# Sixteen widths in steps of 16 slots, in place of eight in steps of 32, for the packed experts' branch trees

## The chip, the core and the metric

The kernel runs on one core of one Trainium2 chip. The metric is the device time of one execution in microseconds (us). All engines of the core are named as in the profile: PE is TensorE's matmul, PEld its weight load, PEq (or PEldq) the sequencer that reads TensorE's instructions, DVE is VectorE, ACT is ScalarE, POOL is GpSimd, SP is SyncE.

## What is computed

The reference is a decoder of two layers on an input of 2 x 1024 rows of 256 numbers, all in float32: a linear attention with a feed-forward block, a latent attention on a context, a recurrent cell, a causal attention, a cross attention, and at the end a mixture of eight experts. The change concerns the experts alone:

```
x = inputs.reshape(G, S, M)                      # 8 groups of 256 rows, M = 256
logits = einsum('GSM,ME->GSE', x, router_w)      # E = 8 experts
dispatch, combine = _gating_top2(logits, C)      # each row goes to 2 experts; C = 64 slots a group and expert
expert_inputs = einsum('GSEC,GSM->EGCM', dispatch, x)
layer_w0 = einsum('EGCM,EMH->EGCH', expert_inputs, w0_kernel)   # H = 1368
layer_w1 = einsum('EGCM,EMH->EGCH', expert_inputs, w1_kernel)
hidden = gelu(layer_w0) * layer_w1
expert_outputs = einsum('EGCH,EHM->EGCM', hidden, wo_kernel)
out = einsum('EGCM,GSEC->GSM', expert_outputs, combine)
```

An expert has 8 x 64 = 512 slots. How many of them hold a row depends on the data, since rows beyond the 64th of a group are dropped and groups may send fewer. Worked out from the reference's inputs, the eight experts fill 512, 512, 323, 393, 421, 337, 340 and 340 slots.

## The kernel before, in words

All work runs on one core, stage after stage, with the order of the instructions of each engine written out in the source (`manual_schedule`: an engine does its instructions in the order in which they were recorded). The last stage is the experts (class `Experts`, from L2432).

`Experts.run` (L2848) loops over the experts e = 0 to 7. For each it does eleven chunks of the hidden width 1368 (ten of 128 and one of 88, `HCH`). A chunk is `hidden`: `up` (L2914) multiplies the expert's inputs by the chunk of w0 and of w1 on TensorE, which gives two products side by side in one PSUM tile `ps_s`; `gelu` on ACT (L2944) reads the first, `mul` on DVE (L2948) multiplies it by the second and writes `hid`. There are two `ps_s` tiles in turn, so `up` of a chunk waits until `mul` of the chunk before the last one is done. After the eleven chunks `turned` transposes the next expert's inputs (L2765, eight small matmuls), and `outputs` (L2957) multiplies `hid` by wo: 44 matmuls, four blocks of 128 slots by eleven chunks. The rows go out to DRAM. wo of the next expert is loaded by SP as soon as the last output is done (L2521, L2522), w0 and w1 of the expert after the next one once the eleven chunks are done (L2513, L2514).

Experts 0 and 1 take all 512 slots. The rows of experts 2 to 6 are packed to the front of their 512 slots, and their number is known only on the chip: `counts` (L2718) reads it into TensorE's registers. So `up` of these experts is written once for each width of a list, `SIZES`, and a tree of branches picks the one to run:

```
L45    SIZES = (256, 288, 320, 352, 384, 416, 448, 512)
...
L2738  def sized(self, value, sizes, emit):
           if len(sizes) == 1:
               emit(sizes[0])
               return
           mid = len(sizes) // 2
           with self.k.tc.If(value > sizes[mid - 1]) as more:
               self.sized(value, sizes[mid:], emit)
           with more.Else():
               self.sized(value, sizes[:mid], emit)
...
L2933  self.sized(self.slots_n[e, 0], SIZES, lambda size: products(lambda t: t[:, :size]))
```

There are 55 such trees, five experts by eleven chunks. In TensorE's program a tree stands as follows: the branches and the bodies one behind the other, the widest body first. A body is 18 instructions: one that waits for the PSUM tile, eight weight loads and eight matmuls (four products, each a float32 matmul in two passes), and a jump to the end of the tree. A tree of eight widths is 7 compares and 8 bodies, 151 instructions; of these a run executes 3 compares and one body, and jumps over the rest. In the first two trees after some borders the waiting instruction is missing, and a body is 17. (`gelu` and `mul` take all 512 slots whatever the width.) Expert 7 has a smaller tree of its own (`WIDTHS`, L46), and the fourth block of the outputs of experts 2 to 6 stands in a single branch (L2888), which runs it if the expert has more than 384 slots; where it is skipped, the sequencer waits there until TensorE has finished what it has.

## Time and profile before

| | us |
|---|---|
| median of the 17 runs (1552.74 to 1563.68) | 1560.18 |
| the execution that was profiled | 1558.33 |
| span of its profile | 1556.5 |
| PE busy in the span | 1508.8 (97%) |
| first matmul of expert 2's trees, from the start of the span | 1265.05 |
| last matmul of expert 6's outputs ends | 1497.52 |
| matmuls L2922 on packed inputs (experts 2 to 7), busy | 172.7 |
| matmuls L2960 (all outputs), busy | 139.8 |

The profile is one execution. Busy time is given for each engine; a "releaser" is what ended an idle time. The float32 matmuls show as two records each, and their ends are modelled, so a record's mean duration is longer than its share of the engine: in a row of back-to-back matmuls the busy time divided by the count is the time that one takes of TensorE. TensorE's branches, waits and loads are the sequencer's; a branch has a record with a duration, but is not counted as busy. In the list of DMA queues, a queue of the kind "instruction" carries the programs of the engines; its queue q8 moved 102 packets of 16384 bytes in this execution. In a DMA answer for a stretch, the second line gives the GB/s in 40 equal slices of the stretch.

### The profile page before, as it was taken

The numbers are of one execution on the slowest core, as the hardware profiler recorded it, in microseconds if no ns is written. First come the engines' busy times: TensorE is split into PE (matmuls) and PEld (weight loads), VectorE is DVE, ScalarE is ACT, GpSimd is POOL, SyncE is SP. The second block draws the span as 40 slices with busy tenths as digits, with TensorE's granted clock in tenths as the row PEclk, the third lists the DMA queues.
The fourth block names the chain that finished last, engine by engine and source line by source line (L and its number), as shares of the span: only waits on it lengthen the run. The fifth ranks groups of instructions, "written<-read, shape, count | busy, mean of one in ns | idle before, by whom it ended". The sixth has DMA issues, their size and how long they took to land. (4 is left out here: it accounts for less than half of the span.)

```text
span 1556.5 us, 21057 instructions
## 1 busy us (share of the span) xinstructions
PE 1508.8 (97%) x8614; PEld 860.4 (55%) x8620; DVE 800.5 (51%) x1470; ACT 510.0 (33%) x782; POOL 288.8 (19%) x303
## 2 busy tenths in 40 slices
PE   7999999999999999999899999999999999999998
PEld 5756555444343344744354444455578476757787
DVE  8812653656554441696667778456762132111243
ACT  2231421433323332315556655644341111111110
POOL 2001320233221320121411111210033100000362
PEclk9999999999999999998899999999999999999999
DMA  6000000000000000010000000035003334232442
GB/s 257 0 0 4 0 0 0 1 1 1 1 0 1 0 31 0 1 36 1 1 1 2 1 1 1 1 128 179 1 33 135 93 135 137 95 105 79 160 143 89
DMA packets 37527, 72.42 MB, mean 47 GB/s; under 512 B 4568, under 2 KB 28312, under 8 KB 37016
## 3 DMA queue, kind: packets, MB, share of 16 engines
q1 hardware_dynamic: 28744, 53.21, 9.8%
q0 software_dynamic: 4704, 13.64, 2.7%
q10 hardware_dynamic: 3952, 3.70, 0.7%
q8 instruction: 102, 1.67, 0.4%
q14 instruction: 25, 0.20, 0.0%
HBM read 55.72 MB, written 14.81 MB: 45 GB/s over the span
## 5 line engine op out<-in xcount | busy, mean ns | idle before, releaser
L2922 PE MATMUL ps_s<-xe,w 128*128 128x352 f32 (+9 forms) x616 | 172.7, 442 | 2.9 <-ACT rows L148 1.8
L1720 PE MATMUL ps_s<-kT,qT 32*128 32x512 f32 (+3 forms) x768 | 163.3, 542 | 6.7 <-DVE mneg L1754 6.1
L2948 DVE TENSOR_TENSOR hid<-ga,ps_s 128x512 f32<-128x512 f32 (+3 forms) x99 | 62.1, 628 | 205.4 <-ACT ga L2944 205.4
L1900 ACT ACTIVATE pT<-ps_t 128x512 f32<-128x512 f32 x244 | 132.3, 595 | 106.7 <-PE ps_t L1834 106.6
L1834 PE MATMUL ps_t<-qT,kT 32*128 32x512 f32 (+3 forms) x656 | 160.9, 536 | 1.5 <-ACT pT L1900 1.4
L2922 PEld LDWEIGHTS ps_s<-xe,w 128*128 128x128 f32 (+1 forms) x616 | 108.3, 188 | 65.1 <-issue 31.7
L2960 PE MATMUL ps_o<-wo,hid 128*128 128x256 f32 (+1 forms) x638 | 139.8, 380 | 0.9 <-DVE hid L2948 0.9
L2960 PEld LDWEIGHTS ps_o<-wo,hid 128*128 128x128 f32 (+1 forms) x638 | 120.6, 190 | 17.9 <-DVE hid L2948 1.4
L2944 ACT ACTIVATE ga<-ps_s 128x512 f32<-128x512 f32 (+3 forms) x99 | 54.3, 549 | 197.5 <-PE ps_s L2922 194.8
L1107 DVE TENSOR_REDUCE part<-ps_s 128x2 f32<-128x1024 f32 x64 | 77.3, 1220 | 61.1 <-PE ps_s L1097 60.4
L1231 ACT ACTIVATE pT<-ps_s 128x1024 f32<-128x1024 f32 x64 | 65.5, 1023 | 114.4 <-PE ps_s L1224 114.4
L1720 PEld LDWEIGHTS ps_s<-kT,qT 32*128 32x128 f32 x768 | 63.0, 191 | 67.0 <-issue 35.6
L1754 DVE TENSOR_REDUCE part<-ps_s 128x2 f32<-128x1024 f32 x64 | 78.1, 1221 | 38.9 <-PE ps_t L1834 36.9
L1798 PE MATMUL ps_o<-pT,vr 128*32 128x256 f32 (+1 forms) x1280 | 92.3, 376 | 1.8 <-ACT oS L1812 1.8
L1847 POOL TENSOR_SCALAR_AFFINE_SELECT pT<-pT 128x512 f32<-128x512 f32 (+1 forms) x80 | 43.9, 551 | 248.6 <-ACT pT L1900 228.9
L1236 POOL TENSOR_TENSOR acc<-acc,pT 128x1024 f32<-128x1024 f32 x24 | 56.4, 2352 | 160.6 <-ACT pT L1231 152.4
L1754 DVE TENSOR_REDUCE mneg<-ps_s 128x2 f32<-128x768 f32 (+2 forms) x96 | 80.5, 867 | 2.2
L2922 PE MATMUL ps_s<-xin,w 128*128 128x256 f32 (+3 forms) x264 | 77.8, 452 | 0.0
L1834 PEld LDWEIGHTS ps_t<-qT,kT 32*128 32x128 f32 x656 | 72.2, 191 | 7.8 <-ACT pT L1900 3.9
L1798 PEld LDWEIGHTS ps_o<-pT,vr 128*32 128x32 f32 x1280 | 27.6, 110 | 81.0 <-issue 68.2
L1097 PE MATMUL ps_s<-kT,qT 64*128 64x512 f32 x256 | 70.3, 635 | 0.8 <-DVE part L1088 0.8
L1151 PE MATMUL ps_o<-pT,vr 128*64 128x512 f32 x256 | 69.4, 624 | 0.9
(453 smaller groups left out, 2318.7 us busy)
## 6 DMA issues: line engine op xcount, KB each, us to landing
w<-in_w SPq DMA_DIRECT2D x32, 684.0 KB, 6.8
wo<-in_wo SPq DMA_DIRECT2D x8, 1280.0 KB, 8.4
xi_rows<-xin SPq DMA_DIRECT2D x1, 3072.0 KB, 14.1
eo_rows<-rows ACTq DMA_DIRECT2D x12, 256.0 KB, 5.2
xr<-xi_rows POOLq DMA_DIRECT2D x6, 512.0 KB, 9.2
w_ffn<-in_w_ffn SPq DMA_DIRECT2D x1, 2304.0 KB, 13.9
x<-in_x SPq DMA_DIRECT2D x4, 512.0 KB, 6.5
w<-in_w_cell SPq DMA_DIRECT2D x2, 1024.0 KB, 16.9
```

What stands on the lines that cost most here:

```text
L1097: self.k.nc.tensor.matmul(s3[:, hh, :], lhsT=self.q[u][rows, qt * P : (qt + 1) * P], rhs=self.kt[u][rows, half * 512 : (half + 1) * 512], ...
L1107: self.k.nc.vector.tensor_reduce(self.part_of(u)[:, half, qt, :], s3, AX.X, ALU.max, negate=True)
L1151: nc.tensor.matmul(self.o[hh * 64 : hh * 64 + 64, :], lhsT=self.vr[b][:, kk, h * 64 : (h + 1) * 64], rhs=pT[:, hh, :], start=first, stop=last,
L1231: nc.scalar.activation(pT, s3, AF.Exp)
L1720: self.k.nc.tensor.matmul(s3[:, hh, at : at + n], lhsT=self.q[u][rows, qt * P : (qt + 1) * P], rhs=self.kt[u][rows, half * 512 : half * 51 ...
L1754: nc.vector.tensor_reduce(out, s3[:, :, at : at + n], AX.X, ALU.max, negate=True)
L1798: nc.tensor.matmul(self.o[hh * 32 : hh * 32 + 32, cols], lhsT=self.vr[b][:, kk, 4 * grp + hh, :], rhs=of(hh), start=fresh, stop=last and n ...
L1834: nc.tensor.matmul(out[:, at : at + n], lhsT=kt[rows, kk * P : (kk + 1) * P], rhs=q[rows, j * 512 + q0 : j * 512 + q0 + n], start=True, st ...
L1900: nc.scalar.activation(pT[:, hh, :], heads[hh], AF.Exp)
L2922: self.k.nc.tensor.matmul(cols(s[:m, i * 512 : (i + 1) * 512]), lhsT=wt[:, kc, at : at + m], rhs=cols(self.inputs[e][:, kc, first : 512]), ...
L2948: self.k.nc.vector.tensor_mul(self.hid[:m, hc, first : first + n], self.act.pop(hc)[:m, :n], self.now.pop(hc)[:m, 512 : 512 + n])
L2960: self.k.nc.tensor.matmul(o, lhsT=self.hid[:n, hc, st * P : (st + 1) * P], rhs=self.to[:n, hc, :], start=(hc == 0), stop=(hc == len(HCH) - 1),
```

## The change

One line is edited, the list of widths:

```
-SIZES = (256, 288, 320, 352, 384, 416, 448, 512)
+SIZES = (256,) + tuple(range(288, 513, 16))
```

The new list has sixteen widths: 256, then 288, 304, 320 and so on to 512. Nothing else differs in the source. In TensorE's program each of the 55 trees now has 15 compares and 16 bodies, 303 instructions where there were 151 (287 where the bodies have no waiting instruction); a run executes 4 compares and one body. From the first tree of expert 2 to the last branch of expert 6's outputs the program grows from 9254 instructions to 17558. The order of the instructions on all other engines is the same.

By their numbers of slots, experts 2 to 6 run these widths:

| expert | slots | width before | width after |
|---|---|---|---|
| 2 | 323 | 352 | 336 |
| 3 | 393 | 416 | 400 |
| 4 | 421 | 448 | 432 |
| 5 | 337 | 352 | 352 |
| 6 | 340 | 352 | 352 |

## The prediction

> **What bounds the kernel now.** I read the page's busy times first, then the groups by line, then the stretch of experts 2 to 6 (1265.05 to 1497.52 us of the span) by width of matmul, in order of time, by its branches and by its DMA queues.

> ```profile
> PE 1508.8 (97%) x8614; PEld 860.4 (55%) x8620; DVE 800.5 (51%) x1470; ACT 510.0 (33%) x782; POOL 288.8 (19%) x303
> ...
> L2922 PE MATMUL ps_s<-xe,w 128*128 128x352 f32 (+9 forms) x616 | 172.7, 442 | 2.9 <-ACT rows L148 1.8
> ```

> TensorE is the bound: 97% of the span, and before the 616 matmuls of the packed experts it idled 2.9 us in all. So a matmul that gets shorter there shortens the kernel, as long as TensorE's instructions arrive. The three widths that ran:

> ```profile
> L2922 PE MATMUL ps_s<-xe,w 128*128 128x352 f32 x240 | 72.1, 460 | 1.2 <-ACT rows L148 1.0 <-issue 0.2
> L2922 PE MATMUL ps_s<-xe,w 128*128 128x448 f32 x80 | 30.2, 539 | 0.0
> L2922 PE MATMUL ps_s<-xe,w 128*128 128x416 f32 x80 | 28.3, 514 | 0.8 <-ACT rows L148 0.8
> ```

> Busy by count gives what one costs TensorE: 300 ns at 352 columns, 354 at 416, 377 at 448, so 0.80 ns a column ((377.5 - 300.4) / 96). In order of time, expert 5's eleven trees are one unbroken run of 88 matmuls (these rows count two records for a float32 matmul), and expert 3's start after a short stall:

> ```profile
> 1309.83 31.06 PE L2922 MATMUL ps_s<-xe,w 128*128 128x416 f32 x88 [0.82 <-ACT rows L148]
> ...
> 1413.57 26.20 PE L2922 MATMUL ps_s<-xe,w 128*128 128x352 f32 x88
> ```

> Now the branches, all of them and then one alone:

> ```profile
> L2744 PEldq COMPARE_BRANCH  x286: 65/122/3234, 1261.2 to 1524.3; - x143
> ...
> L2744 PEldq COMPARE_BRANCH  x1: 1056/1056/1056, 1424.7 to 1424.7; - x1
> ```

> The columns are smallest, median and longest, in ns. The records come in few sizes: 65 for a compare that falls through, 214 for one that jumps, 176 for the jump that leaves a tree (each begins 58 ns after the end of the one before). But ten in experts 2 to 6 took 954 to 3234 ns. They are waits for code: the queue of the kind "instruction" shows as single slices of 27 GB/s, 16384 bytes in 0.6 us, once the weights have passed (window 1413 to 1437 us, the slices begin at 1422.6, 1426.2, 1429.2 and 1432.8):

> ```profile
> GB/s 0 0 0 106 189 270 333 375 336 299 372 389 77 10 22 20 27 0 0 0 0 0 27 0 0 0 0 27 0 0 0 0 0 27 0 0 0 0 0 0
> ...
> q8 instruction: 5, 0.08, 1.4%
> ```

> By the records the packet of 1423.01 landed at 1424.36. The branch of the second line above began at 1424.72 and ended at 1425.78, 1.41 us after that landing; the next packet started at 1426.51, 0.74 us after the branch's end. All ten long waits read so: the branch ends 1.34 to 1.55 us after a landing (1.40 in the middle), and the next packet starts 0.72 to 0.76 us after the branch, two late ones aside that I come back to. So **TensorE's sequencer has the page that it is in and the next one, and asks for a further page only when it enters the next**. A packet took 1.08 us in the mean of the 36 in experts 2 to 6. A page therefore can be had every 0.75 + 1.08 + 1.40 = 3.23 us at best; the nearest two packets of the whole span start 3.05 us apart. Experts 2 to 6 hold 9254 instructions and took 36 packets, so a page is 257 instructions, whether they are run or jumped over.

> Now a tree is 151 instructions, 0.59 pages: 1.9 us of supply, while TensorE works 2.4 to 3.0 us on it. The supply is hidden with 0.5 to 1.1 us to spare a tree, and single long waits are covered by the sequencer's lead of about a tree: the 1056 ns above lie inside expert 5's unbroken run.

> **The change, part by part.**

> Narrower products. Experts 2, 3 and 4 (323, 393, 421 slots) lose 16 columns: 88 x 16 x 0.80 = 1.13 us each, 3.4 us. Experts 5 and 6 (337, 340) keep 352. `gelu` and `mul` don't change.

> One compare more in a tree. It costs 65 + 58 = 123 ns where it falls through and 214 + 58 = 272 where it jumps; by the paths of the five counts a tree pays 0.12 to 0.42 us more. Nearly all of it lies under the sequencer's lead. Without the lead it shows: after a skipped fourth block (L2888, ahead of experts 3 and 6, where TensorE stands empty while the branches run, the 0.82 us above) and after the two groups of transposes in expert 2 (0.18 and 0.40 us idle by "issue"). Four places, at most 0.42 each: I take 1.0 us.

> [...]

> The pages. A tree becomes 303 instructions, 303 / 257 = 1.18 pages, so its supply takes 1.18 x 3.23 = 3.8 us. TensorE would need 2.3 us (336 columns) to 2.9 (432). **The trees become bound by the supply of code.** For one expert: nine trees of 303 and two of 287 are 3301 instructions, 12.8 pages. Two pages are there when it begins (the outputs before are 18 us of work on less than a page), so 11.8 intervals of 3.23 us remain: 38.2 us. Now the five take, from their first matmul to the end of the last, 28.7, 30.8, 33.0, 26.0 and 26.4 us, 144.9 together; then it is 191. The difference is 46 us, and it swallows both parts above: nobody gains from a shorter matmul that waits for its instruction. The outputs (L2960) have no such trees and don't change.

> [...]

> The load of wo. SP issues it at the start of each expert's trees (1280 KB, 8.4 us to landing). In each such window one page came late: its packet started 1.1, 3.8, 0.8, 4.0 and 2.0 us later than 0.75 us after the branch that entered the page before (at 1271.6, 1315.2, 1367.2, 1419.9, 1461.9), 2.3 us in the mean. Today that is covered. Afterwards a window of 8.4 us holds 8.4 / (3.23 + 2.3) = 1.5 such pages: 3.5 us an expert. I take 16 us in all; the bounds are 0 (the lateness was chance) and 5 x 2 x 4 = 40.

> Sum: the profiled execution took 1558.3; 1558.3 + 46 + 16 = 1620. The median of the runs is 1.9 us above that execution, so **1622 us** on its footing. With 3.05 us a page the 46 become 35; with packets of 1.5 us, as the slowest were, 3.65 us a page and 71. With the bounds of wo: 1595 to 1670.

> **The rivals.**

> *The clock falls.* Where TensorE stood empty for 2.4, 2.0, 2.2 and 1.8 us (at 691.4, 512.8, 752.6 and 1005.4) its granted clock went to one half within 4 us, for 17.1, 3.4, 10.2 and 3.4 us; after gaps of 1.4 and 1.2 us (771.3, 1143.2) it didn't.

> ```profile
> 690.00:694.00 4.00, 1.62 (x8) 0.67 (x7) 3.93 (x8) 1.08 (x2) 3.71 (x7) 1.00 0.59 191
> 694.00:711.00 17.00, 16.65 (x80) 9.19 (x79) 11.54 (x15) 4.06 (x8) 2.72 (x6) 0.50 0.00 0
> ```

> The columns end with the granted clock, the DMA share and GB/s. After the change a tree leaves TensorE empty for 3.8 - 2.4 = 1.4 us, below those gaps, but a late page makes it 3 to 5. Half clock costs a tree 4.7 instead of 3.8 us and doubles whatever outputs it reaches: between 2 and 8 us an expert. I expect an episode or two, inside the range; if every expert falls, 10 to 40 us more, 1632 to 1662, at the middle 1650.

> *The supply is quicker when it is pressed.* If a waiting sequencer, or a jump across a border, had two pages fetched at once, only part of the wait would stay: at half the loss, 1560 + 31 = 1591. For it: some packets in the list have no branch wait near them. Against it: under pressure (1461.9 to 1471.4) packets still came 3.06, 3.28 and 3.09 us apart.

> *The narrower products are what counts.* If a page came faster than TensorE uses one up, 2.3 / 1.18 = 1.9 us, the supply would stay hidden: 1560.2 - 3.4 + 1.0 = 1557.8 us, not slower than before, and a little under the 0.2% (3.1 us) that a measurement of this kernel can tell; with all compares hidden 1556.8, just beyond it. No interval in the span is under 3.05 us, which is why I give it little.

> **How the numbers follow.** Supply-bound trees as worked out: 0.70. The clock falling throughout: 0.14. Half of the supply hidden: 0.09. Narrower products alone: 0.07, of which 0.04 within 0.2% and 0.03 faster. The first three are slower by more than 0.2%: 0.93. The forecast is the first case's 1622. The range goes from 1590, which takes in pages at 3.05 us with wo at nothing and touches the third case, to 1660, which takes in the most of the second; the corners left out, with the fourth case, are about 2 in 10.

> **What would show it.** Right: about 134 packets on q8 in place of 102 (17558 / 257 is 32 more), in the trees 3.0 to 3.5 us apart; 341 branch records in place of 286, some fifty over 0.9 us in place of ten; the 88 matmuls of expert 5, with the same width as before, stretched from 26 to 35 to 42 us and broken by about one "issue" gap a tree; PE busy well below 97%, the outputs of an expert still 15 to 19 us. Wrong: packets under 2.5 us apart in the trees, or expert 5's run still at 26 us. If packets are as forecast but TensorE has no gaps, the lead is longer than I read it. If the granted clock shows long halves in the trees, it is the first rival.

## The result, and the profile after

The changed kernel takes 1633.31 us in the median of 8 runs (1628.99 to 1637.89), the kernel before 1559.65 in the median of 46 (1552.14 to 1565.07): a ratio of 1.0474, 95% interval 1.0456 to 1.0492, 73.7 us slower. The profiled execution took 1634.48 us with a span of 1632.7.

The page of the changed kernel, the lines that answer to those of before, and the queue that carries the code:

```profile
PE 1530.1 (94%) x8614; PEld 865.0 (53%) x8620; DVE 802.5 (49%) x1470; ACT 510.1 (31%) x782; POOL 287.6 (18%) x303
...
q8 instruction: 134, 2.20, 0.5%
...
L2922 PE MATMUL ps_s<-xe,w 128*128 128x352 f32 (+11 forms) x616 | 191.1, 465 | 54.7 <-issue 32.3
```

TensorE fell from 97% to 94% of the span. It now idles 54.7 us ahead of the packed experts' matmuls, where it idled 2.9, and 32.3 of that is put down to "issue": nothing that the profile shows held TensorE up. The queue brought 134 pages in place of 102.

Expert 5 runs the same width, 352, in both kernels, so nothing but the program differs. Its eleven trees in order of time, TensorE alone:

```profile
1454.53 4.90 PE L2922 MATMUL ps_s<-xe,w 128*128 128x352 f32 x16
1463.93 9.86 PE L2922 MATMUL ps_s<-xe,w 128*128 128x352 f32 x24 [4.50 <-issue]
1473.97 2.60 PE L2922 MATMUL ps_s<-xe,w 128*128 128x352 f32 x8 [0.18 <-issue]
1477.49 2.60 PE L2922 MATMUL ps_s<-xe,w 128*128 128x352 f32 x8 [0.91 <-ACT ga L2944]
1483.05 6.48 PE L2922 MATMUL ps_s<-xe,w 128*128 128x352 f32 x16 [2.96 <-issue]
1490.15 2.61 PE L2922 MATMUL ps_s<-xe,w 128*128 128x352 f32 x8 [0.62 <-issue]
1493.34 2.57 PE L2922 MATMUL ps_s<-xe,w 128*88 128x352 f32 x8 [0.58 <-issue]
```

One unbroken run of 26.2 us has become seven pieces over 41.4 us: one to three trees of eight matmuls, then a hole. (The hole named after ACT is a wait for code too. The first branch after the tree before it stood for 2.54 us and ended at 1476.53, 1.40 us after a page had landed; the PSUM tile that the next tree needs had been free since 1475.15. The profile names what ended last before the hole's end.)

The DMA of a stretch of these trees, 1470 to 1494 us in slices of 0.6 us, shows the pages:

```profile
GB/s 0 27 0 0 0 0 27 0 0 0 0 0 27 0 0 0 0 27 0 0 0 0 27 0 0 0 0 0 27 0 0 0 0 27 0 0 0 0 27 0
...
q8 instruction: 8, 0.13, 2.2%
```

A page every five or six slices, about 3.2 us, like a clock, with nothing else on the DMA engines. In the trees of all five experts the middle interval between packets is 3.2 us and the shortest 3.01. The five stages, each from its first matmul, with the busy times, the granted clock, the DMA share and GB/s:

```profile
1271.30:1312.50 41.20, 29.56 (x98) 17.68 (x97) 18.25 (x59) 7.04 (x12) 0.00 (x0) 0.96 0.15 45
1329.20:1372.90 43.70, 34.23 (x88) 17.01 (x89) 9.14 (x25) 5.97 (x10) 0.00 (x0) 0.93 0.16 49
1393.20:1434.60 41.40, 35.20 (x89) 16.52 (x89) 6.87 (x10) 6.56 (x11) 0.00 (x0) 0.96 0.15 46
1454.50:1495.70 41.20, 31.45 (x89) 17.93 (x88) 6.87 (x10) 6.56 (x11) 0.00 (x0) 0.88 0.15 45
1512.50:1557.70 45.20, 31.22 (x89) 17.48 (x90) 11.23 (x21) 5.97 (x10) 16.40 (x18) 0.92 0.31 90
```

The second window ends 0.4 us before its last matmul does. With that it is 213.1 us in place of 144.9: 68.2 of the 76.2 us between the two spans. Their lengths hardly follow their widths (336, 400, 432, 352, 352). Of the rest, 6.3 us had passed before the trees began, at 1271.3 in place of 1265.0, in code that is the same in both kernels; across the profiles of this study that start lies anywhere between 1259 and 1272.

### The profile page after: what moved, and what is told of

It is laid out like the page before. It is cut to its first block, busy times and chain, and to the rows that moved or that the text cites. A ratio compares the mean times of both kernels' runs of the same rounds, so it can differ in the third digit from the quotient of the medians.

```text
span 1632.7 us, 21112 instructions
## 1 busy us (share of the span) xinstructions
PE 1530.1 (94%) x8614; PEld 865.0 (53%) x8620; DVE 802.5 (49%) x1470; ACT 510.1 (31%) x782; POOL 287.6 (18%) x303
## 5 line engine op out<-in xcount | busy, mean ns | idle before, releaser
L2922 PE MATMUL ps_s<-xe,w 128*128 128x352 f32 (+11 forms) x616 | 191.1, 465 | 54.7 <-issue 32.3
L2922 PEld LDWEIGHTS ps_s<-xe,w 128*128 128x128 f32 (+1 forms) x616 | 111.7, 198 | 131.5 <-issue 84.4
L2960 PE MATMUL ps_o<-wo,hid 128*128 128x256 f32 (+1 forms) x638 | 139.8, 379 | 0.9 <-DVE hid L2948 0.9
L2960 PEld LDWEIGHTS ps_o<-wo,hid 128*128 128x128 f32 (+1 forms) x638 | 120.4, 190 | 18.1 <-DVE hid L2948 1.4
L2922 PE MATMUL ps_s<-xin,w 128*128 128x256 f32 (+3 forms) x264 | 77.8, 452 | 0.0
L1224 PE MATMUL ps_s<-qT,kT 64*128 64x512 f32 x256 | 68.5, 612 | 1.0 <-DVE part L1107 1.0
## 6 DMA issues: line engine op xcount, KB each, us to landing
w_ffn<-in_w_ffn SPq DMA_DIRECT2D x1, 2304.0 KB, 14.7
```

The source lines that it names most:

```text
L1224: nc.tensor.matmul(s3[:, hh, :], lhsT=self.ones_h[hr, :] if i else kt[hr, kk * P : (kk + 1) * P], rhs=rows[hr, cols] if i else q[hr, cols] ...
L2922: self.k.nc.tensor.matmul(cols(s[:m, i * 512 : (i + 1) * 512]), lhsT=wt[:, kc, at : at + m], rhs=cols(self.inputs[e][:, kc, first : 512]), ...
L2960: self.k.nc.tensor.matmul(o, lhsT=self.hid[:n, hc, st * P : (st + 1) * P], rhs=self.to[:n, hc, :], start=(hc == 0), stop=(hc == len(HCH) - 1),
```

## The experiments

The theory is that a tree waits for its pages of code. The rivals are that the branches that are run cost the time, that the narrower or more numerous bodies do, and that TensorE's clock does.

**The branches alone.** The eight widths of before, asked one after the other:

```
 def sized(...):
-    mid = len(sizes) // 2
+    mid = len(sizes) - 1 if sizes[0] > C else len(sizes) // 2
```

> The eight widths of before, but picked by a chain (widest first) in place of a balanced tree: program length is the same 151 instructions a tree, while experts 2, 5 and 6 run 5 compares, 4 of them jumping (1.21 us of the sequencer by 272 and 123 ns; the tree of sixteen runs 0.8 to 0.9, the tree of eight 0.52). Supply of code: pages are as before, the compares lie under the sequencer's lead, so 1560 us within 5 (a few exposed places at 0.7 each). Rival, the branches that are run cost the time: more than the tree of sixteen, 1630 or above.

1561.92 us, ratio 1.0021 (1.0001 to 1.0041). All branches of this kernel, and then of the changed kernel:

```profile
L2744 PEldq COMPARE_BRANCH  x341: 65/208/3134, 1259.6 to 1525.8; - x171
```

```profile
L2744 PEldq COMPARE_BRANCH  x341: 65/208/6363, 1267.4 to 1600.3; - x171
```

The same number of branches, the same middle, 71 us apart. What differs is the long ones: four of over 0.9 us in the first kernel, 53 in the changed one. The branches that are run are not the cost; what they cost is some 2 us.

**The pages alone.** The widths and the balanced tree of before, with copies of the products in the body that no expert runs here, so that a tree has more instructions and runs the same ones:

```
-lambda size: products(lambda t: t[:, :size])
+lambda size: [products(lambda t: t[:, :size]) for _ in range(10 if size == 512 else 1)]
```

> The eight widths and the balanced tree of before, with nine more copies of the four products in the body of the widest width, which no packed expert runs here (none has over 448 slots): a tree is 295 instructions in place of 151, the same 3 compares and the same products are run. Supply of code: 295 / 257 = 1.15 pages a tree, nearly the 1.18 of sixteen widths, so 1560 + 62 to 75, 1622 to 1635 us. Rival, the branches that are run: no change, 1560. Rival, the narrower products or their number have a price of their own: 1560 too.

1620.98 us, ratio 1.0405 (1.0371 to 1.0439), 61.5 us more than before and 1 us under the lower end of what I expected. Its branches and its pages:

```profile
L2744 PEldq COMPARE_BRANCH  x286: 65/123/6169, 1263.0 to 1585.1; - x143
```

```profile
q8 instruction: 133, 2.18, 0.5%
```

286 branches with the middle of before, 133 pages, and most of the loss: code that is never run makes it. With three and six copies in place of nine:

> As the run with nine dead copies, with three: a tree is 199 instructions, 0.77 pages, 2.50 us of supply against 2.38 (352 columns), 2.8 (416) and 3.0 us (448) of matmuls. Supply of code: just at the border, 1560 to 1572 us. A price per instruction in the program, without a threshold: 62 x 48 / 144 = 21 us, 1580.

> Six dead copies: 247 instructions, 0.96 pages, 3.1 us of supply a tree. Supply of code: experts 2, 5 and 6 (2.38 us of matmuls) lose some 4 us each by 10.5 pages less the first at 3.23 us, expert 3 little, expert 4 nothing, and late pages add up to 3 us an expert: 1570 to 1585 us. A price per instruction without a threshold: 62 x 96 / 144 = 41 us, 1600.

| instructions a tree | pages a tree | pages in the profile | time, us | ratio (95% interval) | five stages, us |
|---|---|---|---|---|---|
| 151 (before) | 0.59 | 102 | 1559.6 | | 145 |
| 199 | 0.77 | 112 | 1575.30 | 1.0115 (1.0080 to 1.0151) | 157 |
| 247 | 0.96 | 122 | 1591.21 | 1.0223 (1.0186 to 1.0259) | 174 |
| 295 | 1.15 | 133 | 1620.98 | 1.0405 (1.0371 to 1.0439) | 199 |

The times are medians; the pages and the five stages are those of the profiled execution, which with 247 instructions was the fastest of its five (1582.42).

Both came out above what I had expected of the supply and a little below a plain price per instruction. I had set TensorE's mean time a tree against the mean supply and forgotten the reserve for a late page. That is my reading of it: with 199 instructions, supply (2.50 us) already exceeds a tree of 352 columns (2.38), and the late pages of each expert, which the kernel before covers, come on top. So one page a tree is no safe limit: 48 instructions more, at 0.77 pages a tree, already cost 15.7 us.

The run with 247 instructions also tells something of the clock. Its stages of experts 4 and 5, in the columns of above:

```profile
1366.30:1399.90 33.60, 33.47 (x91) 16.26 (x90) 6.88 (x10) 6.55 (x11) 0.00 (x0) 1.00 0.20 56
1419.90:1454.10 34.20, 27.90 (x91) 15.78 (x90) 6.88 (x10) 6.55 (x12) 0.00 (x0) 1.00 0.18 55
```

The granted clock was whole in all five stages of this execution, and they are 29 us longer than before. Expert 5 loses 8.2 us, and expert 4, whose tree of 3.0 us just about covers the supply of 3.1, loses 0.5. So the wait for code costs time without any half clock.

**More matmul work in the same pages.** The changed kernel with its sixteen bodies, each multiplying all 512 columns whatever its name:

```
-products(lambda t: t[:, :size])
+products(lambda t: t[:, :512])
```

> The changed kernel with its sixteen bodies left as they are in number and length, but each multiplies all 512 columns. TensorE's work in the trees grows from 113 to 190 us (440 records of 430 ns), 39 us an expert, 3.45 us a tree, still under the 3.8 us of supply. Supply of code: no slower than the changed kernel, 1625 to 1640 us, and no halves of the clock in the trees, since TensorE hardly stands empty; if it is clearly faster, the clock was part of the cost. If matmuls had a part in the trees' time: up to 1633 + 77 = 1710.

1637.14 us, ratio to before 1.0518 (1.0471 to 1.0564), against 1.0474 (1.0456 to 1.0492) for the changed kernel. Its matmuls between 1265 and 1562 us, and the stage of expert 4 with the clock:

```profile
L2922 PE MATMUL ps_s<-xe,w 128*128 128x512 f32 x400 | 182.1, 610 | 21.2 <-issue 6.3 <-DVE c L2784 4.4 <-ACT ga L2944 4.1
```

```profile
1392.30:1434.70 42.40, 38.59 (x89) 15.97 (x88) 6.88 (x10) 6.56 (x11) 0.00 (x0) 1.00 0.16 45
```

TensorE is busy for 200 us of the five stages in place of 162, and the kernel takes 4 us more, less than the two intervals tell apart. In the changed kernel the width of a product has become nearly free; the code's length is what is paid for. The clock ran at one half for 10 us of these stages, where I had expected none, in place of 31 in the changed kernel, and no time came back; but with wider products the trees also have less slack, so this doesn't price the clock.

**Without the load that makes pages late.**

```
 def begin(self, e):
-    self.to = self.load_out(e)
+    self.to = self.to if 2 < e < MOST else self.load_out(e)
```

> The changed kernel without the loads of wo for experts 3 to 6: they multiply by the wo of expert 2 (that part of the result is left out). Supply of code with pages made late by the load of wo: four of the five stages of trees lose their late pages, so 1633 less some 13 to 25, 1608 to 1620 us, no packet in these trees later than 1 us after its due time, and fewer halves of the clock. If the lateness has another cause: 1633. If the clock alone were the cost: 1633 less some 10.

1618.63 us, ratio to before 1.0384 (1.0344 to 1.0424): 14.7 us less than the changed kernel. The DMA at the start of expert 5's trees, 16 us in slices of 0.4 us, first in the changed kernel (from 1454.0), then in this one (from 1442.2):

```profile
GB/s 0 0 0 0 90 228 90 218 312 271 340 320 289 340 389 371 384 387 126 3 10 18 13 0 0 41 0 0 0 0 0 0 0 41 0 0 0 0 0 0
```

```profile
GB/s 0 0 0 0 0 28 340 287 41 0 0 0 0 0 0 41 0 0 0 0 0 0 0 0 41 0 0 0 0 0 0 0 41 0 0 0 0 0 0 0
```

A slice of 41 GB/s is a page; the one before lies just ahead of both windows, at 1453.55 and 1441.76. Above, wo fills the slices from 1455.6 to 1461.6, and the next page came at 1460.9, within them, after 7.39 us. Below it came at 1445.4, after 3.66 us (the slices from 1444.2 are rows going out), and then as regularly as elsewhere. In both the pages after that are some 3.2 us apart. The same interval falls from 6.67 to 3.70 at expert 4 and from 5.07 to 3.37 at expert 6, and stays at 7.17 (6.87) at expert 2, whose wo is still loaded. At expert 3 there was little to lose: 3.94 and 3.56. The late pages are the load's work. In the four stages without it no page came more than 0.8 us late. The halves of the clock went from 31 to 20 us, fewer but not few, so not all of the 14.7 us need be the pages'. The stages here:

```profile
1264.20:1307.00 42.80, 31.66 (x98) 18.94 (x98) 18.27 (x59) 7.03 (x12) 0.00 (x0) 0.88 0.14 44
1323.70:1364.50 40.80, 33.05 (x89) 16.58 (x90) 9.14 (x25) 5.97 (x10) 0.00 (x0) 0.96 0.05 13
1384.30:1422.90 38.60, 33.58 (x89) 15.83 (x89) 6.88 (x10) 6.56 (x11) 0.00 (x0) 1.00 0.05 13
1442.80:1479.50 36.70, 28.18 (x89) 15.53 (x88) 6.88 (x10) 6.56 (x11) 0.00 (x0) 1.00 0.04 13
1496.50:1539.90 43.40, 31.32 (x89) 17.11 (x90) 11.23 (x21) 5.97 (x10) 17.14 (x18) 0.92 0.23 62
```

Experts 4 and 5, with no load and a whole clock, take 38.6 and 36.7 us.

**The same length of program, but in one piece.** The kernel before with 1672 dead instructions after an expert's outputs:

```
+with tc.If(self.slots_n[e, 0] > ROOM - 1):
+    for _ in range(38):
+        self.outputs(part, 3)
```

> The kernel before with 1672 dead instructions an expert in one piece, a branch after the outputs that is never taken, so that TensorE's program is as long as the changed one's but its trees are as before. If pages that are jumped over have to come through in sequence: 6.5 pages of 3.23 us an expert, less the 3.9 us of matmuls that are queued, 17 us an expert, 1645 us and 134 packets. If a long jump fetches its target alone: two misses of 3.2 us an expert and the added branch's wait for TensorE, 1570 to 1590 us and about 105 packets. If only the length of the whole program counted: 1633.

1586.95 us, ratio 1.0176 (1.0127 to 1.0225). The added branches, and the pages:

```profile
L2890 PEldq COMPARE_BRANCH  x5: 3419/3562/3687, 1314.6 to 1523.1; - x5
```

```profile
q8 instruction: 112, 1.84, 0.5%
```

A program as long as the changed one, 27 us slower than before where that one is 74, with 112 pages, ten more than before and not 32. A jump over six pages doesn't bring them in; it fetches where it lands, and stands still 3.4 to 3.7 us for it, five times, with an added wait for TensorE at each. So it is the pages on the sequencer's way that count, and the time in which they are crossed, not the length of the program.

**The narrower products without the pages.** First eight widths, of which the inputs use the changed kernel's:

```
-SIZES = (256, 288, 320, 352, 384, 416, 448, 512)
+SIZES = (256, 320, 336, 352, 400, 432, 448, 512)
```

> Eight widths again, 256, 320, 336, 352, 400, 432, 448 and 512, so that experts 2 to 6 run 336, 400, 432, 352, 352 as in the changed kernel, at the program length of before. Supply of code: pages as before, and the narrower products show at last: 3.4 us less than before, 1556 (as long as the narrower trees, 2.27 us, still cover the 1.9 us of supply). If narrower products bring nothing even so: 1560.

1559.37 us, ratio 0.9995 (0.9976 to 1.0013): the forecast 0.9978 lies inside the interval, and so does nothing at all. The profile tells more: the stages of experts 2, 3 and 4 are 0.6, 0.9 and 1.2 us shorter than before, 5 and 6 the same, 142.2 us in all in place of 145.0.

Then five widths, the same ones and 512, and five that are cut to these inputs. These two ran beside the kernel before on a chip where that one took 1581.31 us:

```
-SIZES = (256, 288, 320, 352, 384, 416, 448, 512)
+SIZES = (336, 352, 400, 432, 512)      # narrow5
+SIZES = (324, 340, 396, 424, 512)      # fit5
```

> The widths that the changed kernel runs, 336, 400, 432, 352, with 512 for the rest: five widths, 94 instructions a tree. Supply of code: 3.4 us less than before, 1556, trees together 141 to 142 us. If narrower products brought nothing: 1559.6.

> Five widths, 324, 340, 396, 424 and 512, cut to the numbers of slots of these inputs (323, 337, 340, 393, 421; 512 stays for any other): a tree is 94 instructions, 0.37 pages, 1.2 us of supply, and experts 2 to 6 lose 28, 20, 24, 12 and 12 columns against the kernel before, 96 x 88 x 0.80 = 6.8 us. Supply of code: the products are the bound again, 1559.6 - 6.8 = 1552 to 1553 us, trees together 138 us in place of 145, no branch over 0.9 us but for a few. If narrower products brought nothing: 1559.6.

The first took 1580.04 us, ratio 0.9997 (0.9974 to 1.0020): 1.3 us less where I had expected 3.4, which settles nothing. In its profile experts 2 to 4 are 0.8, 1.3 and 1.2 us shorter than in the first chip's profile of before and expert 5 the same, but expert 6 takes 35.9 us in place of 26.4. The second took 1573.73, ratio 0.9949 (0.9929 to 0.9969), 8 us less than before and faster than both kernels; the absolute 1552 can't be compared with that chip. Its branches:

```profile
L2744 PEldq COMPARE_BRANCH  x231: 65/176/450, 1268.4 to 1540.4; - x116
```

No branch waits for a page any more (89 pages, and the longest branch is 450 ns). Experts 2 to 5 are 1.5, 1.6, 1.8 and 0.9 us shorter than in the first chip's profile of before, near the 2.0, 1.4, 1.7 and 0.8 of 0.80 ns a column. Expert 6, at 28.1 us, is longer than there. In both runs TensorE stands empty for 6.59 us near the end of expert 6's trees, in the first ahead of the last tree, in the second just behind it:

```profile
1488.16 3.92 PE L2922 MATMUL ps_s<-xe,w 128*88 128x352 f32 x8 [6.59 <-DVE hid L2948]
```

```profile
1492.07 1.97 PE L2765 MATMUL ps_s<-ident,xr 128*128 128x128 f32 x8 [6.59 <-DVE hid L2948]
```

DVE waited there for ACT, and ACT 8.6 us for something that these profiles don't name. The longest branch of the two runs is 0.89 us, so this is no wait for code. There is no profile of the kernel before on that chip, so whether it has this hole too stays open. The list is cut to one set of inputs: it stays right for others, but their counts would fall on its wider entries.

## Why the prediction was right, step by step

**TensorE's sequencer has its page and the next one, and a page takes 3.23 us.** Right: 3.2 us in the middle, 3.01 at the shortest, 134 pages as forecast, and 52 branches of over 0.9 us in the trees of experts 2 to 6, where it said some fifty. Each of the 52 ended 1.33 to 1.53 us after a page had landed, with no other page under way, and the next page started 0.66 us after its end at the earliest. "Whether they are run or jumped over" was too wide: the trees' jumps land in the page they are in or the next, and there it holds; a jump over six pages leaves them out, and costs 3.4 to 3.7 us itself.

**Trees bound by the supply, 38.2 us an expert, +46.** Right in mechanism and near in size. Where neither load nor clock interferes a stage takes 36.7 to 38.6 us. Dead code alone gives 61.5 of the 73.7 us, with eight more instructions a tree still missing.

**The load of wo, +16.** Right: without it for four of the five experts 14.7 us go, some of which may be the clock's. (The 3.5 us an expert that the prediction works out are 17.5 for five, not 16; the difference is small.)

**The clock.** The forecast was an episode or two; the profile has eight stretches of half clock in the trees, of 3.4 or 6.8 us, 31 us in all, at least one in every expert. By the prediction's own sign this is nearer to its first rival than to its first case, and 1633 lies at the lower edge of that rival's 1632 to 1662: the time alone doesn't part the two. Forecast and measurement are 11.7 us apart (73.7 against 62). In the profiled execution the five stages are 68.2 us longer than before, 6.2 over the forecast, and 6.3 us more had passed before the trees, in the same code. If any step was sized too small, this is the one. In the run without wo the stages with halves are the longer ones (40.8 to 43.4 us with, 36.7 and 38.6 without), but they differ in other things too: expert 2 still has its wo, and expert 6 the gather's DMAs. Against it stand the run that nearly freed the clock and was no faster, and experts 4 and 5 of the run with nine dead copies:

```profile
1385.60:1424.10 38.50, 34.83 (x90) 15.65 (x89) 6.89 (x10) 6.56 (x11) 0.00 (x0) 1.00 0.18 53
1444.00:1481.60 37.60, 30.70 (x90) 17.60 (x89) 6.88 (x10) 6.55 (x11) 0.00 (x0) 0.91 0.16 50
```

Expert 5 has 6.8 us of half clock, expert 4 none, and expert 5 is no longer. What the halves cost stays open. That code is the main cost doesn't hang on it: with 247 instructions a tree the stages grow by 29 us with no half clock at all.

The prediction's list of holes and halves also leaves one out. The profile of before has a half of 3.4 us at 1117.4, and in the 16 us ahead of it TensorE stood empty for 0.25 us at most. A hole is not the only thing that such a half follows.

**The added compare.** Costed at nearly nothing under the sequencer's lead; a chain that runs as many branches costs 2.3 us (0.2 to 6.4) without the pages.

**The narrower products, -3.4, swallowed.** Right: 2.8 us in the stages when the code stays short, nothing to be seen in the changed kernel, where even 512 columns add only 4 us.

The rivals "the supply is quicker when pressed" and "the narrower products are what counts" fall with the 3.01 us that no interval in the changed kernel's trees goes below.

## What to carry to other kernels

Before you multiply the variants of a piece of code, count its instructions as a load to be brought in: here a page of 257 of TensorE's instructions can be had every 3.2 us, and code that is jumped over within two pages is paid like code that is run (144 instructions a tree that never run cost 61.5 us). Set that against the time the engine works on the piece, with a reserve for pages made late by a large load; the kernel before showed ten branches of 1 to 3 us, all covered, and 48 instructions a tree more already cost 15.7 us. Sixteen widths at finer steps lost 4.7%; five cut to these inputs won a little (0.9949), and five at the widths that the changed kernel runs nothing that can be told (0.9997).
